# A two-layer Perceiver block on one core: the state-space powers of layer 1's kernel made by VectorE under the end of the first cross-attention

## The chip, the core and the metric

The kernel runs on one core of one Trainium2 chip. A core has engines with queues of their own: PE (TensorE; its weight loads are shown as PEld), DVE (VectorE), ACT (ScalarE), POOL (GpSimd) and SP (SyncE, which here only issues DMAs). They meet through semaphores. The metric is the device time of one execution in microseconds (us); before the change its median over three runs is 2672.54 us.

## The reference, cut to what matters

Two layers, each a cross-attention, a mixing block and a feed-forward block, each added to `x` of 4 x 256 x 256. Three parts matter here.

```python
# layer 0, first block: 16 heads of 16, 256 queries per batch against 4096 context rows
x = x + _L0_xattn_ref(_layernorm(x), ctx_768, ...)       # softmax(q k^T) v, projected
# layer 0, second block: 16 heads of 32, a decayed second-order linear attention
x = x + _L0_attn_ref(_layernorm(x), ...)
# layer 1, first block, contains a state-space convolution whose kernel needs only weights
def s4d(x, log_dt, A_re, A_im, C_re, C_im, D_skip):
    dt = exp(log_dt);  dtA = dt[:, None] * A
    dC = C * (exp(dtA) - 1.0) / A
    powers = exp(dtA[:, :, None] * arange(L))            # L = 256
    K = 2.0 * einsum('dn,dnl->dl', dC, powers).real
```

`K` depends on no activations, so it can be made anywhere ahead of layer 1. The kernel calls "layer 0's" the time in which it makes it; the weights are those of layer 1.

## The kernel before, in words

`program` runs the blocks one after another: `l0_xattn`, `l0_attn`, `l0_ffn`, then layer 1.

`l0_xattn` has 16 units `u`, four batches of four groups of heads. A unit has 16 steps, and each step two halves (`hp` in `step`, two heads each). Two things go on in one step. For unit `u`, PE makes scores (`ps_s`, L444), ACT their exponentials (`e`, L469), and PE adds up values (`o_ps`, L406) in `sums`, one step later. For a unit that is LEAD = 18 steps ahead, PE makes scores in the other layout (`ps_a`, L458) and DVE takes their maxima (`mx`, L473), four `TENSOR_REDUCE`s of 512 columns in a step, two in each half. All of `ps_s` and `ps_a` come from one ring of seven PSUM banks (`ring`); a half takes four of them, in the order score, maxima, score, maxima. A half therefore can't start its scores before the maxima of the half two before it have been read. The last 18 steps have no unit ahead: DVE has only the end of a unit there (`finish`: `o_rec` L173, `on` L174).

Keys and values of a group of eight heads lie in `kts[0]`, `vs[0]` or in `kts[1]`, `vs[1]`; units 14 and 15 use only the second pair. The products that fill them come from `keys` and `values`, which run beside units 0 to 13.

`l0_attn` has 16 units as well. A unit makes scores on PE (`ps_s`, L612), multiplies them by the decay on DVE (`p`, `u`, `z`, L621, six instructions of 768 columns), and makes further products on PE (L632), the last of which ACT copies to `oT` (L641). `first_half` of the next unit is written ahead of `second_half` of this one. Every four units `add_projected` adds to `x`.

Beside these units runs the generator `s4d_kernel`, advanced twice per unit. Its first part makes powers: two exponentials by polynomials, sine and cosine, complex products, and then two tables, `low` (powers 0 to 15) and `high` (16 times as much, with the factor dC), each by four doublings of six instructions, of 128, 256, 512 and 1024 columns. `low` is made by POOL, `high` and everything else by DVE. Its second part makes sums: PE multiplies `low` by `high` (`ps_sn`, L916), DVE masks and reduces (L925, L926), PE transposes (`ps_st`, L937), ACT copies to `s_out`, and SP writes it to `kern`.

Each engine's queue is worked off in order. The order within a queue is not that of the text: the build places instructions by priority and its own estimate of when their inputs and memory are there. (In the trace before, the layer norm of later batches stands among that of the first.) SBUF is handed out in pools; a tile that comes to lie where an older one was waits for the last users of the older one.

The memory for `s4d_kernel` (pool `s4`) is opened after `l0_xattn` and its weights are closed, above that of `l0_ffn`'s weights (`w_f0`).

Of the kernel before, what the change touches and what calls it, by code (L numbers as in the profile page):

```python
# [21 lines left out]
P = 128  # L22
# [222 lines left out]
    return t  # L245


def l0_xattn(c, w):

# [9 lines left out]
    LEAD = 18  # L259
    with ExitStack() as es:  # L260
        one = es.enter_context(tc.tile_pool(name="x0_one", bufs=1))
        ring = es.enter_context(tc.tile_pool(name="x0_ring", bufs=7, space=PSUM))
        acc = es.enter_context(tc.tile_pool(name="x0_acc", bufs=1, space=PSUM))
        two = es.enter_context(tc.tile_pool(name="x0_two", bufs=2))
# [3 lines left out]

        kts, vs, mexps = [], [], []
        for i in range(2):  # L270
            kt = one.tile([P, 2, G], F32, tag=f"kt{i}", name=f"kt{i}")
            kts.append(kt)

            v = one.tile([P, GT * 8 * W + 16], F32, tag=f"v{i}", name=f"v{i}")
            vs.append(v)
            m = one.tile([P, 2, P], F32, tag=f"mexp{i}", name=f"mexp{i}")
            mexps.append(m)
        w.ctxT += [context_keys(c, two, 0, 1), context_keys(c, two, 0, 2, nc.scalar)]
        nc.gpsimd.memset(kts[0][:, 0, :], 1.0)
        mask_rows(c, one, w.mu)  # L280
        nc.vector.memset(kts[0][:, 1, :], 1.0)
# [5 lines left out]
        def keys(b, gp):  # L287

            gs = slice(gp * P, (gp + 1) * P)
            first = (b, gp) == (0, 0)  # L290
            for c4 in range(4):
                ctxT = w.ctxT.pop(0) if w.ctxT else context_keys(c, two, b, c4)
                pss = [bank("ps_k0"), bank("ps_k1")]
                for j, ps in enumerate(pss):
                    nc.tensor.matmul(ps, w.wk[:, 0, gs], ctxT[:, j * 512 : (j + 1) * 512], start=True, stop=False)
                for j, ps in enumerate(pss):
                    hs = slice(64 * j, 64 * j + 64)
                    nc.tensor.matmul(ps, w.wk[hs, 1, gs], ctxT[hs, 1024:1536], start=False, stop=True)  # L298
                ks = two.tile([P, 2, 512], F32, tag="ks", name="ks")
                for j, ps in enumerate(pss):  # L300
                    nc.scalar.copy(ks[:, j, :], ps)  # L301
                for i in range(2):
                    for h in range(4):
                        r = 64 * i + 16 * h
                        ((nc.scalar, nc.gpsimd)[i] if first else nc.sync).dma_start(
                            kts[gp][32 * h : 32 * h + 16, i, c4 * 1024 : (c4 + 1) * 1024],
                            ks[r : r + 16].rearrange("p j n -> p (j n)"),
                        )
                yield

        def values(b, gp):
            v = vs[gp]
            gs = slice(gp * P, (gp + 1) * P)
            for c4 in range(4):
                ctxT = context_keys(c, two, b, c4)
                for i0 in (0, 2):
                    pss = [bank("ps_v0"), bank("ps_v1")]
                    for i in (i0, i0 + 1):
                        ks = slice((i - i0) * P, (i - i0 + 1) * P)
                        for j, ps in enumerate(pss):  # L320
                            k0 = j * 512 + i * P
                            nc.tensor.matmul(ps[:, ks], ctxT[:, k0 : k0 + P], w.wv[:, 0, gs], start=True, stop=False)  # L322
                        for j, ps in enumerate(pss):
                            hs = slice(64 * j, 64 * j + 64)
                            nc.tensor.matmul(  # L325
                                ps[:, ks],
                                ctxT[hs, 1024 + i * P : 1024 + (i + 1) * P],
                                w.wv[hs, 1, gs],
                                start=False,
                                stop=True,  # L330
                            )
# [7 lines left out]

        def tokens(b):  # L340

            xn = row_norm(c, two, "xn", b)
            xnT = two.tile([P, 2, S], F32, tag="xnT", name="xnT")
            ps = bank("ps_t")
            for k in range(2):
                for i in range(2):
# [137 lines left out]
        for t in range(-LEAD, n):  # L484
# [55 lines left out]
def l0_attn(c, w, beside):  # L540
# [9 lines left out]
    with ExitStack() as es:  # L550
# [109 lines left out]
            z = masked_scores(q, wt, 0, "z")  # L660
            return summed([(nu, p), (v, z)], f"oT{u % 4}")

        beside = beside(psum)
        rows = {}
        late = first_half(0)
        oTs = []
        for u in range(16):
            nxt = first_half(u + 1) if u + 1 < 16 else None
# [4 lines left out]
            if u % 4 == 3:  # L673
                add_projected(c, psum, u // 4, oTs, w.wo)
                oTs = []
        for _ in beside:
            pass

def l0_ffn_weights(c, pool):
    w = Ctx()
    w.ga = load_k(c, pool, "f0_ga")
    w.wi = load_k(c, pool, "f0_wi")
    w.wo = load_k(c, pool, "f0_wo")
# [2 lines left out]
    w.bg = load_bc(c, pool, "f0_bg")  # L690
    w.bo = load_bc(c, pool, "f0_bo")
    w.iota = load_bc(c, pool, "iota8")
    return w


def l0_ffn(c, w):
# [111 lines left out]
    v.tensor_tensor(o1, o1, tmp, ALU.add)  # L808


def s4d_kernel(c, pool, psum):

# [16 lines left out]
    ldt = new("ldt")  # L829
    for half in range(2):  # L830
        nc.sync.dma_start(ldt[64 * half : 64 * half + 64, :], c.a["s4_ldt"][half].partition_broadcast(64))
    skip = load(c, pool, "s4_skip", [32, 8])
    own = load(c, pool, "s4_own", [P, P])
    dt = exp_less(c, pool, ldt, 0.0, n2, "s4x")
    re, im = pair("dta")
    v.tensor_tensor(re, ar, dt, ALU.mult)
# [42 lines left out]

    yield  # L880
    low, high = new("low", ns), new("high", ns)
    tmps = [new("tl", [P, 16, 8, 8]), new("th", [P, 16, 8, 8])]

    def groups(t):
        return t.rearrange("p (g e) -> p g e", e=8)

    for i in range(2):
        v.tensor_tensor(high[:, i, :, 0, :], groups(q[i]), groups(n), ALU.mult)
        nc.gpsimd.memset(low[:, i, :, 0, :], 1.0 - i)  # L889
    zs = [pair(f"z{i}") for i in range(9)]  # L890
    zs[0] = z
    for lev in range(8):
        m = 1 << (lev % 4)
        t = low if lev < 4 else high
        if lev == 4:
            v.tensor_scalar(zs[4][1], zs[4][1], -1.0, None, ALU.mult)
        cmul(
            nc.gpsimd if lev < 4 else v,
            [t[:, i, :, m : 2 * m, :] for i in range(2)],
            [t[:, i, :, 0:m, :] for i in range(2)],  # L900
            [groups(p).unsqueeze(2).to_broadcast([P, 16, m, 8]) for p in zs[lev]],
            tmps[lev // 4][:, :, 0:m, :],
        )
# [984 lines left out]
def program(tc, a, out):  # L1888
# [3 lines left out]
    with ExitStack() as es:  # L1892
# [15 lines left out]


        with tc.tile_pool(name="w_a0", bufs=1) as pool_a0:  # L1910
            with tc.tile_pool(name="w_x0", bufs=1, side="right") as pool:
                w = l0_xattn_weights(c, pool)
                l0_xattn(c, w)
                w_a0 = l0_attn_weights(c, pool_a0)
            pool_f0 = es.enter_context(ExitStack())
            w_f0 = l0_ffn_weights(c, pool_f0.enter_context(tc.tile_pool(name="w_f0", bufs=1, side="right")))
            with tc.tile_pool(name="s4", bufs=1, side="right") as pool:
                l0_attn(c, w_a0, partial(s4d_kernel, c, pool))

        with ExitStack() as stack:  # L1920
            w = l1_context_keys(c, stack)
# [145 lines left out]
```

## Time and profile before

| what | value |
|---|---|
| three runs | 2669.84, 2672.54, 2682.69 us |
| profiled execution, time / span | 2677.02 / 2674.9 us |
| mean granted PE clock | 0.929 |
| PE busy, share of the span | 2420.3 us, 90% |
| DVE busy, share of the span | 1618.9 us, 61% |
| ACT busy, share of the span | 1095.0 us, 41% |
| POOL busy, share of the span | 179.1 us, 7% |
| `l0_xattn`, last maxima to last value sum | about 1213.5 to 1276.7 us |
| `l0_attn`, first norm to last addition | about 1276.7 to 1577 us |

Stages are given in microseconds from the start of the span. In the timeline a row has the start, the duration, the engine, the line, the operation with its tiles and a count, and in brackets the idle time ahead of it and what ended it. A row of the table of windows has the window, its length, the busy time of PE, PEld, DVE, ACT and POOL with the number of instructions in parentheses, the granted PE clock (1.00 is full), the DMA share and GB/s. Durations of neighbours on DVE overlap by some 0.08 us, so the cost of one instruction in a full queue is the distance from its start to the next start.

### The profile page before, as it was taken

What the parts mean: (1) busy time and instruction counts of PE and PEld (TensorE: products, weight loads), DVE (VectorE), ACT (ScalarE), POOL (GpSimd) and SP (SyncE); (2) the same over time, 40 slices, a digit from 0 to 9 for tenths busy, and PEclk for the clock granted to TensorE, in tenths of its full rate; (3) what the DMA queues carried; (4) which work ended last, traced back from release to release, by engine and by line L of the source; (5) the groups of instructions that cost most, each with busy time, mean ns of one, the idle gap of its engine ahead of it and who ended that gap; (6) DMA issues with size and microseconds to landing.
All of it is one profiled execution on the core that took longest, in us unless ns stands there. A gap on an engine that the chain in (4) does not pass through costs nothing. (4 is left out here: it accounts for less than half of the span.)

```text
span 2674.9 us, 47755 instructions
## 1 busy us (share of the span) xinstructions
PE 2420.3 (90%) x19345; PEld 1419.5 (53%) x19345; DVE 1618.9 (61%) x3881; ACT 1095.0 (41%) x1913; POOL 179.1 (7%) x202
## 2 busy tenths in 40 slices
PE   8999999999999999999768989888999898984896
PEld 4445454545545454544435544466776777453554
DVE  6655655565565655561784440898798892735554
ACT  1355555555455555556111211555555562010221
POOL 3000000000000000000030000001010011412000
PEclk7899999999999999999888999799999999996876
DMA  7221213121221212100100012210303012100110
GB/s 197 76 53 58 61 50 80 38 73 45 62 56 55 63 37 73 45 2 1 43 1 1 5 47 67 79 60 20 99 22 97 6 50 96 55 0 16 33 24 8
DMA packets 63186, 130.78 MB, mean 49 GB/s; under 512 B 11584, under 2 KB 38912, under 8 KB 62512
## 3 DMA queue, kind: packets, MB, share of 16 engines
q1 hardware_dynamic: 61344, 123.73, 16.4%
q8 instruction: 154, 2.52, 0.4%
q10 hardware_dynamic: 1104, 2.88, 0.4%
q0 software_dynamic: 512, 1.05, 0.2%
q14 instruction: 72, 0.59, 0.1%
HBM read 97.12 MB, written 5.34 MB: 38 GB/s over the span
## 5 line engine op out<-in xcount | busy, mean ns | idle before, releaser
L473 DVE TENSOR_REDUCE mx<-ps_a 128x1 f32<-128x512 f32 x1024 | 658.3, 686 | 436.1 <-PE ps_a L458 436.1
L469 ACT ACTIVATE e<-ps_s 128x512 f32<-128x512 f32 x1024 | 555.8, 594 | 382.5 <-PE ps_a L458 356.5
L458 PE MATMUL ps_a<-kt,qa 32*128 32x512 f32 x2048 | 636.2, 653 | 1.9 <-DMA kt<-ks 0.8
L444 PE MATMUL ps_s<-qb,kt 32*128 32x256 f32 x4096 | 585.9, 401 | 0.0
L444 PEld LDWEIGHTS ps_s<-qb,kt 32*128 32x128 f32 x4096 | 348.7, 184 | 212.4 <-issue 94.2
L406 PE MATMUL o_ps<-e,v 128*32 128x256 f32 x4096 | 327.6, 391 | 0.0
L1152 PEld LDWEIGHTS ps_w<-diag,e 128*128 128x128 f32 x2048 | 238.8, 197 | 23.5 <-issue 21.5
L1152 PE MATMUL ps_w<-diag,e 128*128 128x128 f32 x2048 | 244.5, 281 | 0.4 <-POOL diag L1139 0.4
L458 PEld LDWEIGHTS ps_a<-kt,qa 32*128 32x128 f32 x2048 | 220.6, 186 | 20.9 <-DVE mx L473 7.8
L1109 DVE MAX8 cand<-sc 128x8 f32<-128x128 f32 x1024 | 212.2, 275 | 8.7 <-ACT sc L1097 8.7
L406 PEld LDWEIGHTS o_ps<-e,v 128*32 128x32 f32 x4096 | 81.0, 108 | 239.5 <-issue 229.5
L1133 DVE SCALAR_TENSOR_TENSOR e<-sc,top,e 128x1024 f32<-128x1024 f32 x128 | 159.1, 1279 | 28.5 <-ACT e L1124 28.5
L1124 ACT ACTIVATE e<-sc,neg 128x1024 f32<-128x1024 f32 x128 | 143.1, 1147 | 33.3 <-PE ps_w L1152 29.1
L1097 ACT COPY sc<-ps_s 128x1024 f32<-128x1024 f32 x128 | 126.3, 1007 | 41.9 <-PE ps_s L1088 39.6
L1166 PEld LDWEIGHTS ps_c<-cx,wT 128*128 128x128 f32 x512 | 86.1, 196 | 27.2 <-ACT wT L1160 11.3
L1166 PE MATMUL ps_c<-cx,wT 128*128 128x193 f32 x512 | 97.1, 341 | 1.9 <-ACT wT L1160 1.9
L335 ACT COPY v<-ps_v 128x256 f32<-128x256 f32 x128 | 41.4, 375 | 137.0 <-PE ps_v L325 137.0
L322 PE MATMUL ps_v<-x_wv,ctxT 128*128 128x128 f32 x512 | 92.8, 305 | 0.0
L322 PEld LDWEIGHTS ps_v<-x_wv,ctxT 128*128 128x128 f32 x512 | 69.4, 195 | 35.3 <-DVE mx L473 21.8
L1088 PE MATMUL ps_s<-kt,q 32*128 32x512 f32 x512 | 85.4, 647 | 0.0
L889 POOL MEMSET s_low<- 128x128 f32 x2 | 0.3, 206 | 1241.1 <-DVE x L188 1241.1
L301 ACT COPY ks<-ps_k 128x512 f32<-128x512 f32 x64 | 34.4, 589 | 111.4 <-PE ps_k L298 97.7
(403 smaller groups left out, 2735.6 us busy)
## 6 DMA issues: line engine op xcount, KB each, us to landing
ctxT<-in_ctxT SPq DMA_DIRECT2D x78, 768.0 KB
kt<-ks SPq DMA_DIRECT2D x352, 64.0 KB
cx<-in_ctx SPq DMA_DIRECT2D x16, 768.0 KB
x_w<-in_x_w SPq DMA_DIRECT2D x2, 1024.0 KB
qk<-rot SPq DMA_DIRECT2D x8, 256.0 KB
a_qk<-qk SPq DMA_DIRECT2D x16, 128.0 KB
ctxT<-in_ctxT ACTq DMA_DIRECT2D x2, 768.0 KB
x<-in_x SPq DMA_DIRECT2D x4, 256.0 KB
```

The source lines that it names most:

```text
L322: nc.tensor.matmul(ps[:, ks], ctxT[:, k0 : k0 + P], w.wv[:, 0, gs], start=True, stop=False)
L406: nc.tensor.matmul(o_pss[u][32 * h : 32 * h + 32, :S], vs[g // 2][:, c0 : c0 + 32], ew[h][:, n % 2, :], start=(n == 0), stop=(n == GT - 1),)
L444: nc.tensor.matmul(ps[:, k * S : (k + 1) * S], kts[u % 4 // 2][hs, u % 2, ks], qbs[u][hs, :], start=True, stop=True,)
L458: nc.tensor.matmul(ps, qas[u][hs, tt * P : (tt + 1) * P], kts[u % 4 // 2][hs, u % 2, ch * 512 : (ch + 1) * 512], start=True, stop=True,)
L469: nc.scalar.activation(e, ps.rearrange("p (k n) -> p k n", k=2), AF.Exp)
L473: nc.vector.tensor_reduce(mxs[u][:, tt, h, ch : ch + 1], ps, AX.X, ALU.max)
L1097: nc.scalar.copy(t, ps)
L1109: nc.vector.max(cands[u][:, n, :], sc[u][c4][:, i // 4, (i % 4) * P : (i % 4 + 1) * P])
L1124: nc.scalar.activation(t, src, AF.Exp, bias=neg)
L1133: nc.vector.scalar_tensor_tensor(t, src, top[:, 31:32], t, ALU.is_ge, ALU.mult)
L1152: nc.tensor.matmul(ps[:, i * P : (i + 1) * P], e[c4][:, half, i * P : (i + 1) * P], diag, start=(h == 0), stop=(h == 3),)
L1166: nc.tensor.matmul(ps_c[:, : DC + 1], wT[:, i * P : (i + 1) * P], cxs[b][t][:, j, :], start=(n == 0), stop=(n == 31))
```

## The change

`s4d_kernel` is cut in two. `s4d_powers` makes the tables and is advanced in the last 18 steps of `l0_xattn`; `s4d_sums` runs beside the first units of `l0_attn`. The products of `low` move from POOL to DVE, as do the two `memset`s. So that the tables have memory, `kts[0]`, `vs[0]`, the context, key and norm tiles move to two pools on the right side, which are closed in unit 14 at step 4, and pool `s4` is opened there. The weights of `l0_ffn` are loaded when the sums are done, no longer ahead of `l0_attn`. In `l0_attn` the generator is made after `first_half(0)`, and is no longer run to its end behind the units.

```diff
-def l0_xattn(c, w):
+def l0_xattn(c, w, beside):
...
+        early = es.enter_context(ExitStack())
+        first = early.enter_context(tc.tile_pool(name="x0_first", bufs=1, side="right"))
+        proj = early.enter_context(tc.tile_pool(name="x0_proj", bufs=2, side="right"))
...
-            kt = one.tile([P, 2, G], F32, tag=f"kt{i}", name=f"kt{i}")
+            pool = (first, one)[i]
+            kt = pool.tile([P, 2, G], F32, tag=f"kt{i}", name=f"kt{i}")
...
-            v = one.tile([P, GT * 8 * W + 16], F32, tag=f"v{i}", name=f"v{i}")
+            v = pool.tile([P, GT * 8 * W + 16], F32, tag=f"v{i}", name=f"v{i}")
...
+            if u == 14 and kp == 4:
+                early.close()
+                tail = beside()
+            if ua >= 16 and ka % 2 == 0:
+                next(tail, None)
...
         for _ in range(2):
             sums(0)
+        for _ in tail:
+            pass
...
-        beside = beside(psum)
         rows = {}
         late = first_half(0)
+        beside = beside(psum)
...
-        for _ in beside:
-            pass
...
-def s4d_kernel(c, pool, psum):
+def s4d_powers(c, pool, w):
...
-    tmps = [new("tl", [P, 16, 8, 8]), new("th", [P, 16, 8, 8])]
+    tmps = new("tl", [P, 16, 8, 8])
...
-        nc.gpsimd.memset(low[:, i, :, 0, :], 1.0 - i)
+        v.memset(low[:, i, :, 0, :], 1.0 - i)
...
         cmul(
-            nc.gpsimd if lev < 4 else v,
+            v,
...
-            tmps[lev // 4][:, :, 0:m, :],
+            tmps[:, :, 0:m, :],
         )
+        if m > 2:
+            yield
         if lev < 7:
             cmul(v, zs[lev + 1], zs[lev], zs[lev], tmp)
-        yield
+    yield
+
+    w.low, w.high = low, high
+
+
+def s4d_sums(c, pool, w, psum):
...
-            with tc.tile_pool(name="w_x0", bufs=1, side="right") as pool:
-                w = l0_xattn_weights(c, pool)
-                l0_xattn(c, w)
-                w_a0 = l0_attn_weights(c, pool_a0)
+            pool_x0 = es.enter_context(ExitStack())
+            w = l0_xattn_weights(c, pool_x0.enter_context(tc.tile_pool(name="w_x0", bufs=1, side="right")))
             pool_f0 = es.enter_context(ExitStack())
-            w_f0 = l0_ffn_weights(c, pool_f0.enter_context(tc.tile_pool(name="w_f0", bufs=1, side="right")))
-            with tc.tile_pool(name="s4", bufs=1, side="right") as pool:
-                l0_attn(c, w_a0, partial(s4d_kernel, c, pool))
+            pools, w_s4, w_f0 = [], Ctx(), Ctx()
+
+            def powers():
+                pools.append(pool_x0.enter_context(tc.tile_pool(name="s4", bufs=1, side="right")))
+                return s4d_powers(c, pools[0], w_s4)
+
+            def sums(psum):
+                yield from s4d_sums(c, pools[0], w_s4, psum)
+                pool_x0.close()
+                l0_ffn_weights(c, pool_f0.enter_context(tc.tile_pool(name="w_f0", bufs=1, side="right")), w_f0)
+
+            l0_xattn(c, w, powers)
+            l0_attn(c, l0_attn_weights(c, pool_a0), sums)
```

More of the change, by code (lines that the diff above doesn't have):

```diff
@@ L277, in l0_xattn @@
             mexps.append(m)
-        w.ctxT += [context_keys(c, two, 0, 1), context_keys(c, two, 0, 2, nc.scalar)]
+        w.ctxT += [context_keys(c, proj, 0, 1), context_keys(c, proj, 0, 2, nc.scalar)]
         nc.gpsimd.memset(kts[0][:, 0, :], 1.0)
@@ L289, in keys @@
             gs = slice(gp * P, (gp + 1) * P)
-            first = (b, gp) == (0, 0)
+            start = (b, gp) == (0, 0)
             for c4 in range(4):
-                ctxT = w.ctxT.pop(0) if w.ctxT else context_keys(c, two, b, c4)
+                ctxT = w.ctxT.pop(0) if w.ctxT else context_keys(c, proj, b, c4)
                 pss = [bank("ps_k0"), bank("ps_k1")]
@@ L298, in keys @@
                     nc.tensor.matmul(ps, w.wk[hs, 1, gs], ctxT[hs, 1024:1536], start=False, stop=True)
-                ks = two.tile([P, 2, 512], F32, tag="ks", name="ks")
+                ks = proj.tile([P, 2, 512], F32, tag="ks", name="ks")
                 for j, ps in enumerate(pss):
@@ L304, in keys @@
                         r = 64 * i + 16 * h
-                        ((nc.scalar, nc.gpsimd)[i] if first else nc.sync).dma_start(
+                        ((nc.scalar, nc.gpsimd)[i] if start else nc.sync).dma_start(
                             kts[gp][32 * h : 32 * h + 16, i, c4 * 1024 : (c4 + 1) * 1024],
@@ L314, in values @@
             for c4 in range(4):
-                ctxT = context_keys(c, two, b, c4)
+                ctxT = context_keys(c, proj, b, c4)
                 for i0 in (0, 2):
@@ L340, in tokens @@
         def tokens(b):
-            xn = row_norm(c, two, "xn", b)
-            xnT = two.tile([P, 2, S], F32, tag="xnT", name="xnT")
+            xn = row_norm(c, proj, "xn", b)
+            xnT = proj.tile([P, 2, S], F32, tag="xnT", name="xnT")
             ps = bank("ps_t")
@@ L675, in l0_attn, with l0_ffn_weights @@
                 oTs = []
-        for _ in beside:
-            pass
-def l0_ffn_weights(c, pool):
-    w = Ctx()
+def l0_ffn_weights(c, pool, w):
     w.ga = load_k(c, pool, "f0_ga")
@@ L692, in l0_ffn_weights @@
     w.iota = load_bc(c, pool, "iota8")
-    return w
 def l0_ffn(c, w):
@@ L831, in s4d_kernel @@
         nc.sync.dma_start(ldt[64 * half : 64 * half + 64, :], c.a["s4_ldt"][half].partition_broadcast(64))
-    skip = load(c, pool, "s4_skip", [32, 8])
-    own = load(c, pool, "s4_own", [P, P])
+    w.skip = load(c, pool, "s4_skip", [32, 8])
+    w.own = load(c, pool, "s4_own", [P, P])
     dt = exp_less(c, pool, ldt, 0.0, n2, "s4x")
@@ L901, in s4d_kernel, with new @@
             [groups(p).unsqueeze(2).to_broadcast([P, 16, m, 8]) for p in zs[lev]],
-            tmps[lev // 4][:, :, 0:m, :],
+            tmps[:, :, 0:m, :],
         )
+        if m > 2:
+            yield
         if lev < 7:
             cmul(v, zs[lev + 1], zs[lev], zs[lev], tmp)
-        yield
+    yield
+    w.low, w.high = low, high
+def s4d_sums(c, pool, w, psum):
+    nc = c.nc
+    v = nc.vector
+    low, high, own, skip = w.low, w.high, w.own, w.skip
+    def new(name, shape):
+        return pool.tile(shape, F32, tag="s4_" + name, name="s4_" + name)
     sums = new("sums", [P, 2, 16, 16])
```

## The prediction

> **What bounds the kernel now.** I read, in this order, the costliest groups of the page, the table of windows around the change, and the timelines of DVE, PE and ACT there.
>
> ```profile
> L473 DVE TENSOR_REDUCE mx<-ps_a 128x1 f32<-128x512 f32 x1024 | 658.3, 686 | 436.1 <-PE ps_a L458 436.1
> ```
>
> In the cross-attention the maxima wait for PE: 436.1 us of idle DVE stand ahead of them. PE sets the pace, and DVE has room in small pieces. How much, the windows show: unit 15's maxima, the 18 steps behind them, units 0 to 4 of the attention (the powers), units 5 to 8 (the sums), units 9 to 12 (nothing beside them).
>
> ```profile
> 1168.00:1213.50 45.50, 44.70 (x500) 21.70 (x500) 33.30 (x54) 27.14 (x50) 0.00 (x0) 1.00 0.01 2
> 1213.50:1276.70 63.20, 61.81 (x597) 31.81 (x598) 2.58 (x3) 39.72 (x74) 0.00 (x0) 1.00 0.00 1
> 1276.70:1401.50 124.80, 86.79 (x724) 51.95 (x723) 104.59 (x244) 17.60 (x41) 29.67 (x26) 0.81 0.08 24
> 1401.50:1485.60 84.10, 72.08 (x665) 45.18 (x664) 34.54 (x44) 13.95 (x29) 0.00 (x0) 0.84 0.00 1
> 1485.60:1544.30 58.70, 52.90 (x530) 31.76 (x529) 23.36 (x27) 11.95 (x28) 0.00 (x0) 0.94 0.03 6
> ```
>
> While unit 15's maxima run, DVE is busy for 33.3 of 45.5 us: 12 us are free. In the 18 steps behind them it is busy for 2.6 of 63.2 us: 60 us are free. In the attention with the powers DVE is busy for 104.6 of 124.8 us and PE only for 86.8: DVE bounds that stretch.
>
> **The change: where the powers land.** The text advances them in the last 18 steps. The built program doesn't have them there. In its DVE queue the first power stands behind the 12th of unit 15's 64 maxima and the last in front of the 55th; behind the 64th there is none. The powers are ready as soon as unit 13 lets go of `kts[0]` and `vs[0]`, and the build places them there as filler. This is one half of a step in that queue (in rows from left to right, names shortened):
>
> ```
> L478 TensorReduce mx<-ps_a     L812 tl<-low,z1 128x256     L478 TensorReduce mx<-ps_a
> L813 low<-low,tl 128x256       L814 low<-low,z1 128x256     L815 tl<-low,z1 128x256
> L812 tmp<-z1 128x128           L816 low<-low,tl 128x256     L813 z2<-z2,tmp 128x128
> L814 z2<-z1 128x128            L815 tmp<-z1 128x128         L811 low<-low,z2 128x512
> L478 TensorReduce mx<-ps_a     L478 TensorReduce mx<-ps_a
> ```
>
> A queue is worked off in order, so each pair of maxima now waits for the powers in front of it. PE can't outrun them: a half needs the banks of the maxima two halves back (ring of seven, four a half). So 21 halves run at DVE's pace. Everything in PE's queue (scores, value sums) waits with them.
>
> **Cost of it.** The spacing of maxima and of powers in a full queue:
>
> ```profile
> 1202.68 1.29 DVE L473 TENSOR_REDUCE mx<-ps_a 128x1 f32<-128x512 f32 x2 [0.61 <-PE ps_a L458]
> 1204.32 1.29 DVE L473 TENSOR_REDUCE mx<-ps_a 128x1 f32<-128x512 f32 x2 [0.35 <-PE ps_a L458]
> ...
> 1305.17 0.22 DVE L779 TENSOR_SCALAR s_k<-s_dta 128x128 f32<-128x128 f32 x1
> 1305.30 0.22 DVE L779 TENSOR_SCALAR s4x_k<-s4x_x 128x128 f32<-128x128 f32 x1
> ...
> 1368.14 0.42 DVE L806 TENSOR_TENSOR s_high<-s_high,s_z 128x256 f32<-128x256 f32 x1
> 1368.48 0.42 DVE L805 TENSOR_TENSOR s_high<-s_high,s_th 128x256 f32<-128x256 f32 x1
> 1368.81 0.28 DVE L804 TENSOR_TENSOR s_tmp<-s_z 128x128 f32<-128x128 f32 x1
> 1369.02 0.42 DVE L807 TENSOR_TENSOR s_th<-s_high,s_z 128x256 f32<-128x256 f32 x1
> ```
>
> From start to start: 0.135 us with one tensor input, 0.20 with two (1368.81 to 1369.02), 0.335 at 256 columns; the same timeline gives 0.60 at 512 and 1.13 at 1024, and 0.12 more where an instruction needs the one right ahead of it. The built queue holds 24 of the first kind (3.4 us), 117 of the second (24.0), 12 each of 256, 512 and 1024 columns (4.1, 7.2, 13.6), a reciprocal (0.9) and two memsets (0.2, estimated as one-input instructions), and 26 that need their neighbour (3.1): 56.4 us of powers. The 24 instructions of `low` are in it; POOL needed up to 2.47 us for one of 1024 columns, DVE 1.21.
>
> The 42 maxima of these 21 halves take 0.606 us each (pair 1.29, less the overlap): 25.5 us. Unit 13's reciprocal and product stand among them, 2.0 us. Sum 83.9 us, or 4.0 a half. Before, a half took 1.77 us (1168.24 to 1211.40 is about 24 of them), 37.2 us for 21. Added: 46.7 us. PE's run-ahead gives back one half, 1.8. The eight loads of s4 tables now go out when PE releases `vs[0]`, about 1163.6; with the starts 0.4 us apart and 2.4 us to land, as `s_ldt` had, they land about when they are needed, 1169: 0 to 4 us, I take 1. A cold clock behind the stretch: 1. **Loss 47 us**, of which none is hidden: the 18 steps behind it are bounded by PE (61.8 of 63.2 us) and run as before, with DVE idle.
>
> Two rules bear on this sum. The Trainium skill, "VectorE: DVE Perf Modes", section "The DRAIN you can't avoid", lets the next instruction start only when the one before has left the pipe; then each costs its whole duration, powers 67.7 and maxima 28.8, and the loss is 61. The rows above show starts 0.08 us ahead of the end before, so I take the row and keep 61 for the range. "TensorE: Matmul & The Clock Gate", section "A second HAM failure mode: psum-queue depth-cycling", says that short waits on PSUM banks in each round make the clock fall to one half and back. This trace shows 0.54 in the five microseconds from 1340, where PE waits for DVE. In the stretched halves it would double PE's 1.77 us to 3.54, still below DVE's 4.0: it adds nothing there, by rule or row, but 3 us more if DVE's shortest halves (3.1 us) meet it.
>
> **Gain in the attention.**
>
> ```profile
> 1354.95 2.42 DVE L803 TENSOR_TENSOR s_high<-s_high,s_z 128x128 f32<-128x128 f32 x1
> ...
> 1364.33 1.07 PE L632 MATMUL ps_oT<-z,vn 128*32 128x256 f32 x4 [11.96 <-DVE z L621]
> ```
>
> Beside POOL's products a DVE instruction of 128 columns takes 2.42 us where it takes 0.28 alone, and PE stands for 11.96 us behind a `z` that is queued after such. All this goes. The ends of units 0, 4, 8, 12 and 15 before:
>
> ```profile
> 1322.25 0.37 ACT L641 COPY oT<-ps_oT 128x256 f32<-128x256 f32 x1 [1.20 <-PE ps_oT L632]
> ...
> 1401.10 0.37 ACT L641 COPY oT<-ps_oT 128x256 f32<-128x256 f32 x1 [3.81 <-PE ps_oT L632]
> ...
> 1485.25 0.37 ACT L641 COPY oT<-ps_oT 128x256 f32<-128x256 f32 x1 [3.81 <-PE ps_oT L632]
> ...
> 1543.91 0.37 ACT L641 COPY oT<-ps_oT 128x256 f32<-128x256 f32 x1 [3.81 <-PE ps_oT L632]
> ...
> 1573.35 0.37 ACT L641 COPY oT<-ps_oT 128x256 f32<-128x256 f32 x1 [3.81 <-PE ps_oT L632]
> ```
>
> Four units with nothing beside them take 58.7 us (1485.25 to 1543.91). Unit 0 without powers: PE has both first halves' scores done by 1305.6 and needs 7.2 more, as unit 4 did from 1394.3 to its copy: 1312.8 instead of 1322.3. Then three times 58.7, then 29.4 as before: 1518.3. The sums (PE, DVE, ACT) move from units 5 to 8 to units 0 to 3 and cost what they did, 1485.25 less 1401.10 less 58.7, 25.5 us: 1543.8, a gain of 29.6. Of the 25.5, some 8 were a half-rate clock (0.53 to 0.50 from 1405 to 1420); if that stays away the gain is 37.6. **I take 34.** Bounds: 22, if the sums' two rounds back to back in unit 0 and again in unit 1 close the gate more often, and 42.
>
> **At nothing:** POOL's queue loses 26 instructions and nothing in it waits. The eight loads of `l0_ffn`'s weights, 2.3 MB, move on SP from 1280 to behind the write of `kern`, about 1390; SP has nothing else before 1576, when they are wanted, and before they took about 10 us. Without that cover they would cost those 10. Pools on the other side issue nothing.
>
> **Sum.** +47 - 34 = +13 us. The profiled execution took 2677.0 (span 2674.9), 4.5 above the median; the difference is put on the median: 2672.5 + 13 = **2686 us**. About 0.5%, 13.4 us, is what a measurement of this kernel can tell from no change, so this lies on the edge of it.
>
> **Rivals.** (A) The powers fill DVE's gaps for nothing and the gain stays: 2672.5 - 34 = 2638, faster. For it: DVE has 12 + 60 us free. Against: the 60 lie behind the 64th maximum, where the built queue has no power. It would win if less than about 12 us of powers stood among the maxima; 56 do. (B) DVE costs whole durations, or PE at half clock binds as well: loss 61, 2700. For it: the rule. Against: the rows' overlap. (C) The attention gives little: its PE is near its bound once DVE is out, and the dense sums bring the half clock with them: gain 20, 2700. For it: clock 0.84 in the window of the sums. Against: 38 us of idle PE in the window ahead of that. (D) The change doesn't do what it says: that is the forecast itself, since the powers aren't in the last 18 steps.
>
> **Numbers.** Forecast 0.60, A 0.07, B 0.17, C 0.16. The forecast's own range is 2674 to 2697 (loss 42 to 55, gain 28 to 42), half of it over 2686, none under 2659: 0.30 same, 0.30 slower. B and C are slower. So faster 0.07, same 0.30, slower 0.63. The range leaves out A and the far end of B and C together: 2668 to 2706.
>
> **What would show it.** Right: from about 1164 to 1249 DVE has no idle time, pairs of maxima stand 4 us apart instead of 1.77, PE is busy for less than half (or at half clock); the last 18 steps start at about 1260 instead of 1213.5 and take 63 us again; no POOL products; in the attention units 1 to 4 with the sums take about 76 us (79 before with the powers), units 5 to 8 about 59 (84 before). Wrong: idle DVE among the maxima (loads late, or powers waiting for each other), a PE that keeps its 1.77 us, or sums that make the first units as long as before.

## The result, and the profile after

The changed kernel takes 2682.9 us (median), the kernel before, measured beside it, 2673.4. The ratio is 1.003, 95% interval 1.0018 to 1.0042: 5 to 11 us slower, a small loss where I had forecast 13. Some executions of several kernels below take 30 to 50 us longer, with the 18 steps at half the clock where one of them was traced (e6, e12); the ratios leave these out, unless all executions of a kernel are like that (e1).

The spans of the two profiled executions are 2674.9 and 2681.1 us, 6.2 apart. Two large terms of opposite sign lie under this. The first is in the cross-attention. This is the table of windows of the changed kernel. The rows are: the maxima of unit 15 with the powers among them, its last maxima, the 18 steps behind, units 0 to 4 of the attention, units 5 to 8, units 9 to 12.

```profile
1169.20:1249.70 80.50, 76.93 (x401) 23.18 (x400) 78.75 (x219) 21.79 (x41) 0.00 (x0) 0.58 0.01 3
1249.70:1263.10 13.40, 12.34 (x104) 5.73 (x103) 7.52 (x14) 5.43 (x10) 0.00 (x0) 0.74 0.01 1
1263.10:1326.50 63.40, 62.01 (x599) 31.97 (x598) 2.77 (x4) 39.73 (x74) 0.00 (x0) 1.00 0.00 1
1326.50:1440.80 114.30, 95.35 (x868) 60.21 (x867) 55.51 (x107) 21.47 (x45) 0.00 (x0) 0.91 0.09 25
1440.80:1495.00 54.20, 48.77 (x525) 29.83 (x524) 23.29 (x27) 10.99 (x26) 0.00 (x0) 1.00 0.01 1
1495.00:1552.60 57.60, 52.17 (x527) 31.46 (x526) 23.35 (x27) 11.01 (x27) 0.00 (x0) 0.94 0.00 1
```

DVE is busy for 78.8 of 80.5 us in the first row and for 2.8 of 63.4 in the third: the powers run where the built queue has them, and the 18 steps still have DVE idle. The clock of the first row is 0.58. In the timeline of DVE the maxima stand one by one or in pairs between the powers, and nothing waits but for 1.02 us at 1171, where a table (`ldt`) is still on its way:

```profile
1169.19 1.28 DVE L478 TENSOR_REDUCE mx<-ps_a 128x1 f32<-128x512 f32 x2
1171.49 0.23 DVE L795 TENSOR_SCALAR s4x_x<-s_ldt 128x128 f32<-128x128 f32 x1 [1.02 <-DMA s_ldt<-in_s_ldt]
...
1201.52 0.68 DVE L478 TENSOR_REDUCE mx<-ps_a 128x1 f32<-128x512 f32 x1
1202.12 0.41 DVE L812 TENSOR_TENSOR s_tl<-s_low,s_z 128x256 f32<-128x256 f32 x1
1202.45 0.68 DVE L478 TENSOR_REDUCE mx<-ps_a 128x1 f32<-128x512 f32 x1
...
1203.39 0.42 DVE L814 TENSOR_TENSOR s_low<-s_low,s_z 128x256 f32<-128x256 f32 x1
1203.72 0.42 DVE L815 TENSOR_TENSOR s_tl<-s_low,s_z 128x256 f32<-128x256 f32 x1
...
1251.48 1.29 DVE L478 TENSOR_REDUCE mx<-ps_a 128x1 f32<-128x512 f32 x2 [1.00 <-PE ps_a L463]
1255.06 1.29 DVE L478 TENSOR_REDUCE mx<-ps_a 128x1 f32<-128x512 f32 x2 [2.30 <-PE ps_a L463]
...
1262.26 0.22 DVE L389 TENSOR_REDUCE mexp<-mx 128x8 f32<-128x64 f32 x1
```

`mexp` is where DVE takes the largest of a unit's maxima, once all 64 of its `mx` instructions are done. From unit 14's `mexp` to unit 15's it is 111.9 us (1150.32 to 1262.26), where it was 63.7 (1149.03 to 1212.72): a loss of **48.2 us**. The rows of 1251 and 1255 show the half clock still costing after the powers have ended: now the maxima wait for PE.

Across the whole program the group of the maxima hardly changes, 432.8 us of idle DVE ahead of them instead of 436.1. The cost of this change can't be read from that row, only from the stage:

```profile
L478 DVE TENSOR_REDUCE mx<-ps_a 128x1 f32<-128x512 f32 x1024 | 658.7, 685 | 432.8 <-PE ps_a L463 431.9
```

The other term is in the attention. These are the ends of units 0, 4, 8, 12 and 15 in the timeline of ACT, and ahead of them the reciprocal that ends the cross-attention (DVE's timeline):

```profile
1326.24 1.76 DVE L173 RECIPROCAL o_rec<-den 128x256 f32<-128x256 f32 x1 [49.53 <-PE den L171]
```
```profile
1368.92 0.37 ACT L653 COPY oT<-ps_oT 128x256 f32<-128x256 f32 x1 [3.87 <-PE ps_oT L644]
...
1440.38 0.37 ACT L653 COPY oT<-ps_oT 128x256 f32<-128x256 f32 x1 [3.81 <-PE ps_oT L644]
...
1494.64 0.37 ACT L653 COPY oT<-ps_oT 128x256 f32<-128x256 f32 x1 [3.81 <-PE ps_oT L644]
...
1552.18 0.37 ACT L653 COPY oT<-ps_oT 128x256 f32<-128x256 f32 x1 [3.81 <-PE ps_oT L644]
...
1581.63 0.37 ACT L653 COPY oT<-ps_oT 128x256 f32<-128x256 f32 x1 [3.81 <-PE ps_oT L644]
```

From the reciprocal to the last copy it is 255.4 us, where it was 296.7 (1276.70 to 1573.35): a gain of **41.3 us**. The 18 steps between the two terms take 64.0 us in both. With the 1.3 us by which unit 14's `mexp` already came later, 1.3 + 48.2 - 41.3 = 8.2, which is, but for rounding, how much later the last copy comes. Behind it the changed execution makes up 2.1.

These are two single executions, and the second term varies from one to the next. The stretch takes 63.7 us in all six traces without powers in it, and 111.1 to 111.9 in three with all of them. The attention takes 286.0 to 296.7 us in the five traces that have the code before (those of e7, e8, e9 and e12 with it) and 248.6 to 255.4 in the five that have the changed code (e1, e2, e5, e11). The trace before is the slowest of its five and the changed one the slowest of its own; between the means, 289.9 and 251.6, the gain is 38 us.

### The profile page after: what moved, and what is told of

Its sections match the earlier page's. It is cut to its first block, busy times and chain, and to the rows that moved or that the text cites. A ratio compares the mean times of both kernels' runs of the same rounds, so it can differ in the third digit from the quotient of the medians.

```text
span 2681.1 us, 47776 instructions
## 1 busy us (share of the span) xinstructions
PE 2448.3 (91%) x19345; PEld 1418.8 (53%) x19345; DVE 1611.2 (60%) x3907; ACT 1094.6 (41%) x1913; POOL 148.9 (6%) x176
## 3 DMA queue, kind: packets, MB, share of 16 engines
q1 hardware_dynamic: 61344, 123.73, 16.6%
## 5 line engine op out<-in xcount | busy, mean ns | idle before, releaser
L478 DVE TENSOR_REDUCE mx<-ps_a 128x1 f32<-128x512 f32 x1024 | 658.7, 685 | 432.8 <-PE ps_a L463 431.9
L463 PE MATMUL ps_a<-kt,qa 32*128 32x512 f32 x2048 | 672.5, 670 | 7.1 <-DVE mx L478 3.4
L449 PE MATMUL ps_s<-qb,kt 32*128 32x256 f32 x4096 | 606.6, 412 | 0.0
L449 PEld LDWEIGHTS ps_s<-qb,kt 32*128 32x128 f32 x4096 | 355.2, 188 | 220.0 <-issue 91.4
L411 PE MATMUL o_ps<-e,v 128*32 128x256 f32 x4096 | 336.0, 400 | 0.0
L1177 PEld LDWEIGHTS ps_w<-diag,e 128*128 128x128 f32 x2048 | 238.8, 197 | 23.5 <-issue 21.5
L463 PEld LDWEIGHTS ps_a<-kt,qa 32*128 32x128 f32 x2048 | 230.0, 190 | 38.8 <-DVE mx L478 23.8
L1191 PEld LDWEIGHTS ps_c<-cx,wT 128*128 128x128 f32 x512 | 86.1, 196 | 27.2 <-ACT wT L1185 11.4
L772 POOL TENSOR_TENSOR x<-x,f_bo 128x256 f32<-128x256 f32 x8 | 5.8, 724 | 1645.3 <-DVE x L771 1618.1
```

Of the source, the lines that this page charges most:

```text
L411: nc.tensor.matmul(o_pss[u][32 * h : 32 * h + 32, :S], vs[g // 2][:, c0 : c0 + 32], ew[h][:, n % 2, :], start=(n == 0), stop=(n == GT - 1),)
L449: nc.tensor.matmul(ps[:, k * S : (k + 1) * S], kts[u % 4 // 2][hs, u % 2, ks], qbs[u][hs, :], start=True, stop=True,)
L463: nc.tensor.matmul(ps, qas[u][hs, tt * P : (tt + 1) * P], kts[u % 4 // 2][hs, u % 2, ch * 512 : (ch + 1) * 512], start=True, stop=True,)
L478: nc.vector.tensor_reduce(mxs[u][:, tt, h, ch : ch + 1], ps, AX.X, ALU.max)
L1177: nc.tensor.matmul(ps[:, i * P : (i + 1) * P], e[c4][:, half, i * P : (i + 1) * P], diag, start=(h == 0), stop=(h == 3),)
L1191: nc.tensor.matmul(ps_c[:, : DC + 1], wT[:, i * P : (i + 1) * P], cxs[b][t][:, j, :], start=(n == 0), stop=(n == 31))
```

## The experiments

Three questions: is the loss the place of the powers; what is the gain made of; and, after the first run, why that run gave so little. For the runs in the table the trace gives three stages: the stretch (unit 14's `mexp` to unit 15's), the 18 steps (`mexp` to the last reciprocal) and the attention (reciprocal to the last `oT`).

| kernel | stretch | 18 steps | attention | median us | ratio to before (95%) |
|---|---|---|---|---|---|
| before | 63.7 | 64.0 | 296.7 | 2673.4 | 1 |
| changed | 111.9 | 64.0 | 255.4 | 2682.9 | 1.003 (1.0018 to 1.0042) |
| e1, gate at `mexp` | 64.3 | 101.0 | 252.3 | 2670.7 | 0.9992 (0.998 to 1.0003) |
| e2, upper levels gated | 96.3 | 64.0 | 253.0 | 2672.9 | 0.9984 (0.9968 to 1.0) |
| e3, low table on DVE | 63.7 | 64.0 | 289.8 | 2660.7 | 0.9953 (0.9935 to 0.9972) |
| e4, sums late | 111.6 | 64.0 | 250.3 | 2682.8 | 1.0033 (1.0019 to 1.0046) |
| e5, gate behind unit 14 | 64.3 | 65.7 | 248.6 | 2630.9 | 0.9845 (0.9826 to 0.9863) |
| e10, e5 with sums late | 64.3 | 65.7 | 247.3 | 2631.1 | 0.984 (0.9823 to 0.9858) |
| e11, as e5, gate later | 64.3 | 64.0 | 248.8 | 2632.7 | 0.9853 (0.9836 to 0.9871) |

The median of e2 is over all 14 executions; that of its nine shorter ones (see there) is 2668.6.

**Putting the powers where the text says (e1).**

```diff
     ldt = new("ldt")
...
+    v.scalar_tensor_tensor(ldt, m15[:, 0, :], 0.0, ldt, ALU.mult, ALU.add)
```

`m15` is unit 15's `mexp`, handed to `beside()`. The generator's body first runs behind `with_largest(15)`, so that this is the final `mexp`.

> The changed kernel with one instruction more: behind its load, the first table of the powers is multiplied and added with 0 times unit 15's largest maxima (mexp), so that no power can start before unit 15's 64th maximum. Theory (the loss is the powers' place among the maxima, 48.2 us from the first maximum of unit 15 to mexp; the gain in the attention, 41.3 us, is another matter): the stretch falls back to 60 us, the 18 steps behind it stay at 63 to 65 us because their DVE was idle for 49.5 us in one piece and the powers need 56 of 63, and the time is 2682.9 - 48 = 2635 us, faster than both kernels. Rival 1 (powers slow PE wherever they stand, by the clock or because they overrun the 63 us and hold up unit 14's and 15's ends): the 18 steps grow by 15 us or more, 2650 to 2665. Rival 2 (the loss is the memory given up early, or the loads): nothing changes, 2683.

Measured: the stretch is back at 64.3 us, which answers rival 2: neither the memory given up early nor the loads cost anything there. But the time is 2670.7 us, not 2635. The 18 steps grew to 101 us, the direction of rival 1. Their windows:

```profile
1223.00:1233.00 10.00, 8.30 (x74) 4.03 (x74) 9.69 (x40) 4.95 (x10) 0.00 (x0) 1.00 0.01 2
1233.00:1243.00 10.00, 10.00 (x64) 4.85 (x64) 10.00 (x39) 4.00 (x8) 0.00 (x0) 0.58 0.00 1
1243.00:1253.00 10.00, 10.00 (x56) 4.35 (x56) 10.00 (x18) 3.49 (x7) 0.00 (x0) 0.50 0.01 2
...
1283.00:1293.00 10.00, 10.00 (x58) 4.28 (x51) 0.00 (x0) 4.20 (x8) 0.00 (x0) 0.50 0.00 0
...
1303.00:1313.00 10.00, 10.00 (x62) 4.23 (x58) 0.00 (x0) 3.25 (x6) 0.00 (x0) 0.50 0.00 0
1313.00:1323.00 10.00, 4.50 (x20) 3.38 (x19) 7.22 (x29) 1.95 (x4) 0.00 (x0) 0.84 0.00 0
```

The clock falls to 0.50 at about 1235 and stays there to 1313, long after the powers have ended (1272). PE counts as busy all that time, with half the matmuls in a row. Ahead of the fall PE had three pauses. The first two, 0.81 us behind `mexp` at 1213 and 0.92 us at 1224, are in the kernel before as well. The third is new: in the timeline of PE,

```profile
1224.85 0.70 PE L171 MATMUL den<-o_sb,sel 128*128 128x256 f32 x2 [0.92 <-ACT o_sb L169]
...
1231.85 1.13 PE L449 MATMUL ps_s<-qb,kt 32*128 32x256 f32 x6 [0.78 <-DVE o_rec L173]
```

Unit 14's reciprocal stood behind 16 us of powers in DVE's queue and ran at 1230.04, 16.6 us behind `mexp` instead of 12.2. It is what frees the bank of `den` in the ring, and PE wanted that bank at 1231.1.

**The same without the late reciprocal (e5).**

```diff
     v.tensor_tensor(im, ai, dt, ALU.mult)
     yield
+    yield
+    for t in (re, im):
+        v.scalar_tensor_tensor(t, ons[-1][:, 0:P], 0.0, t, ALU.mult, ALU.add)
```

`ons[-1]` is unit 14's product `on`; the gate of e1 stays.

> The gated kernel again, with one more gate: the first 5.5 us of the powers (up to dta) wait for mexp as before, the other 50 us for unit 14's product on, so that they stand behind unit 14's reciprocal in VectorE's queue instead of in front of it. Theory (in the first gated kernel the half clock from 1235 to 1313 was set off by PE's third pause in 20 us, 0.78 us behind the late reciprocal): without that pause the clock stays at 1.00, the last 18 steps take 63 us instead of 101, the time is 2670.7 - 38 = 2633 us, and the powers end about 1273, ahead of the attention. Rival (56 us of VectorE work beside PE brings the half clock by itself, wherever the reciprocal stands): clock 0.50 again, 2670.

```profile
1223.00:1233.00 10.00, 10.00 (x99) 5.21 (x100) 9.68 (x42) 6.01 (x12) 0.00 (x0) 1.00 0.01 2
1233.00:1243.00 10.00, 10.00 (x100) 5.22 (x102) 9.69 (x44) 6.73 (x14) 0.00 (x0) 1.00 0.01 2
1243.00:1253.00 10.00, 10.00 (x102) 5.22 (x100) 10.00 (x27) 6.73 (x13) 0.00 (x0) 1.00 0.01 2
...
1263.00:1273.00 10.00, 10.00 (x106) 4.94 (x103) 9.97 (x24) 6.52 (x12) 0.00 (x0) 1.00 0.01 2
```

2630.9 us, ratio 0.9845: faster than both kernels. DVE is as full of powers as in e1, PE keeps its 100 matmuls in 10 us and its clock. The powers are hidden but for 1.7 us: the last one, started at 1275.51, holds unit 15's reciprocal up to 1276.65. So the loss of the change is the place of the powers, and in none of e5's five executions did DVE work beside PE bring the half clock by itself.

**Which part of e1 brought it (e7, e8, e9, e12, e11).** e7, e8, e9 and e12 add to the kernel before only idle DVE work between `mexp` and unit 14's reciprocal, and force the reciprocal behind it. The sizes in the list are all that differs.

```diff
                 with_largest(ua)
+                if ua == 15:
+                    t = kts[0][:, 0, 0:1024]
+                    nc.vector.scalar_tensor_tensor(t[:, 0:P], mexps[1][:, 0, :], 0.0, t[:, 0:P], ALU.mult, ALU.add)
+                    for n in [P] * 5 + [1024] * 11:
+                        nc.vector.tensor_tensor(t[:, 0:n], t[:, 0:n], t[:, 0:n], ALU.max)
...
     rec = pool.tile([P, S], F32, tag="o_rec", name="o_rec")
+    if behind is not None:
+        nc.vector.tensor_copy(rec, behind)
```

> The kernel before, with idle VectorE work alone added: a chain of 17 in-place maxima on a free table behind mexp, some 16.5 us, and unit 14's reciprocal put behind it, which is where it stood in the first gated kernel. The powers stay in the attention. Theory (a pause of PE under 1 us behind the late reciprocal sets off the half clock): PE at 0.50 from about 1235 to the end of the cross-attention, 2674 + 38 = 2712 us. Rival (the pause is nothing; the powers' own work did it): the pause alone, 2674 to 2676.

e7 missed its own question. Its reciprocal ran from 1230.63 to 1232.39, but in this build the ring hands PE the bank one half step later, at 1232.5. No pause arose, and 2671.3 us (0.999, 0.9978 to 1.0003) say only that a late reciprocal without a pause costs nothing.

> The kernel before with the idle VectorE chain made 0.86 us longer (17 maxima of which the last has 640 columns), because in the run with the shorter chain unit 14's reciprocal ended 0.15 us before PE needed the bank, so that no pause arose and nothing was tested. Now PE should pause for about 0.75 us at 1232.5, third of three pauses in 20 us as in the first gated kernel. Theory (this pause sets off the half clock for the rest of the 18 steps): 2674 + 38 = 2712 us, in all or most executions. Rival (the pause alone is nothing; powers beside PE, or their order, did it): 2672 to 2676, clock 1.00.

> The same with a chain 2.5 us longer still: PE should pause for 1.6 us at about 1234.2. Theory: half clock to the end of the 18 steps, 2713 us; if the shorter pause left the clock alone and this one doesn't, the length of the pause decides. Rival (no pause of this size matters): 2674 to 2678.

The two pauses, in the timelines of PE of e8 and of e9:

```profile
1233.39 1.13 PE L446 MATMUL ps_s<-qb,kt 32*128 32x256 f32 x8 [0.69 <-DVE o_rec L175]
```
```profile
1236.67 1.13 PE L446 MATMUL ps_s<-qb,kt 32*128 32x256 f32 x8 [1.58 <-DVE o_rec L175]
```

e8: 2672.0 us (0.9996, 0.9982 to 1.001), no half clock in the traced execution, and none of its 20 executions is over 2691: a pause of 0.69 us at that place did nothing, against my theory. e9: the traced execution keeps its clock behind 1.58 us of pause, but three of its eight executions, which were not traced, take 2701 to 2711 us and the others 2666 to 2679.

> The kernel before with a chain of 47 small dependent VectorE instructions of 128 columns between mexp and unit 14's reciprocal, in place of the long ones, so that PE pauses for 0.8 to 1.0 us at the place where it did in the first gated kernel, 6.2 us behind den, and not 7.2 or 9.2 us behind it. No powers beside it. Reading A (the place decides: two pauses of 0.8 us or more within 8 us set off the half clock): 2712 us in all or most executions. Reading B (the pause alone is not enough at any place, it takes the powers that go on behind it): 2674 to 2676 us, clock 1.00.

e12 (`[P] * 46`) puts the pause about where e1 had it. Of 13 executions 12 take 2664 to 2675 us and one 2707. It is the one that was traced, first PE's timeline, then the windows:

```profile
1230.03 1.69 PE L446 MATMUL ps_s<-qb,kt 32*128 32x256 f32 x8 [1.00 <-DVE o_rec L175]
```
```profile
1220.00:1230.00 10.00, 8.10 (x78) 3.82 (x74) 9.05 (x26) 5.69 (x11) 0.00 (x0) 1.00 0.01 2
1230.00:1240.00 10.00, 9.97 (x54) 4.96 (x56) 0.42 (x1) 3.25 (x6) 0.00 (x0) 0.52 0.00 0
1240.00:1250.00 10.00, 10.00 (x56) 4.41 (x58) 0.00 (x0) 3.33 (x7) 0.00 (x0) 0.50 0.01 2
...
1300.00:1310.00 10.00, 10.00 (x54) 4.52 (x52) 0.00 (x0) 3.26 (x6) 0.00 (x0) 0.50 0.00 0
```

The fall comes right behind the pause, with DVE idle from there on, and lasts to the end of the 18 steps (102 us). So a pause can do it with no power beside it, but here only once in 13.

> The first gated kernel with its order of VectorE work kept up to 1227 us (dense powers from mexp on), then unit 14's reciprocal, and the rest of the powers gated behind its product: the reciprocal is 3 us late, but ends about 2 us before PE wants the bank, so PE has no third pause. The two kernels before with a pause alone (0.69 us: clock 1.00 in all executions; 1.58 us: three of eight executions some 35 us longer) leave two readings. Reading 1 (the pause is needed, the powers beside it lower the threshold): clock 1.00, 2631 us. Reading 2 (dense powers from mexp on, or the late reciprocal itself, bring the half clock, the pause is no part of it): clock 0.50, 2670 us.

e11 moves e5's second gate from behind `dta` to behind the sine and cosine, so that DVE's queue is e1's up to 1227 us and the reciprocal is still late, but early enough for PE. In DVE's timeline:

```profile
1229.45 0.23 DVE L861 TENSOR_SCALAR s_cs<-s_cs 128x128 f32<-128x128 f32 x1
1229.59 1.75 DVE L173 RECIPROCAL o_rec<-den 128x256 f32<-128x256 f32 x1
1231.45 0.42 DVE L174 TENSOR_TENSOR on<-o_sb,o_rec 128x256 f32<-128x256 f32 x1
```

Its `mexp` is at 1215.86, 2.4 us after e1's, so this reciprocal is 2.9 us earlier relative to it than e1's, and 1.6 us later than in the kernel before. The clock is 1.00 through all 18 steps, and they take 64.0 us; 2632.7 us, ratio 0.9853, the same as e5. Reading 1 fits: with DVE full of powers but no third pause, none of the 14 executions of e5, e10 and e11 is over 2640 us. All 14 of e1 (2664 to 2675 us) lie some 40 us above e5's; in the two traces 35.3 of these are in the 18 steps and 3.7 in the attention.

A third pause is not needed for the fall, though. e6 (below) has the changed kernel's cross-attention, with nothing on DVE in the 18 steps, and its trace caught a fall. PE's timeline, then the windows:

```profile
1259.40 0.44 PE L394 MATMUL ps_m<-ident,mexp 128*128 128x128 f32 x2 [1.06 <-DVE mexp L389]
```
```profile
1255.00:1260.00 5.00, 3.94 (x44) 1.91 (x43) 3.47 (x7) 2.66 (x6) 0.00 (x0) 1.00 0.01 3
1260.00:1265.00 5.00, 5.00 (x34) 2.23 (x34) 0.30 (x1) 2.17 (x4) 0.00 (x0) 0.60 0.00 0
...
1275.00:1280.00 5.00, 4.51 (x22) 2.07 (x20) 1.33 (x1) 1.36 (x3) 0.00 (x0) 0.50 0.02 3
```

Here the clock falls at about 1261, behind the ordinary pause at unit 15's `mexp`. The changed kernel makes the same pause (1.06 us, at 1262.5) and kept its clock in its trace.

What stays open is what decides. Executions 30 to 50 us longer were 0 of 20, 3 of 8 and 1 of 13 with a late pause without powers (e8, e9, e12), and the powers that go on behind it, or its exact instant, made it 14 of 14 in e1. Where the trace has no third pause, they were 1 of 19 in the changed kernel, 3 of 7 in e6, 5 of 14 in e2, none of 16 in e4, and none of 127 in the kernel before. In all three traces with a fall in the 18 steps it comes 0.5 to 2.8 us behind a pause of 0.78 to 1.06 us. So such a pause can set it off, and taking e1's third pause away cured e1; a rule for when it does is not shown.

**Half a dose (e2).**

```diff
             v.tensor_scalar(zs[4][1], zs[4][1], -1.0, None, ALU.mult)
+            for z4 in zs[4]:
+                v.scalar_tensor_tensor(z4, m15[:, 0, :], 0.0, z4, ALU.mult, ALU.add)
```

> The changed kernel with the same gate put only on the upper levels (the table z of level 4), so that some 17 us of the 56 us of powers stand behind mexp and 39 us stay among the maxima. Theory (the loss is proportional to the DVE time among the maxima): 39 us at the measured density of 2.7 us a half fill 14.6 halves, each 2.2 us longer than PE's pace, loss 33 instead of 48, time 2668 us. Rival (a cost for entering the stretch: loads, half clock, one wait): the loss stays above 43, 2678 to 2683.

The stretch takes 96.3 us, 32.7 more than before; 33 were expected. The loss goes with the DVE time among the maxima, and is not a fixed price for entering the stretch. The ratio, 0.9984 against the changed kernel's 1.003, is 12 us less; 15 were expected. Five of the 14 executions take 2715 to 2717 us, some 47 us more than the others. None of these was traced.

**What the gain is made of (e3, e6, e4).**

e3 is the kernel before with the low table's products on DVE (`nc.gpsimd if lev < 4 else v` becomes `v`) and its two memsets.

> The kernel before with one part of the change alone: the 24 products of the low table and its two memsets on VectorE instead of GpSimd, in the first attention's units as before. Theory (the gain in the attention comes from taking the powers out of it; contention is a part): DVE keeps the powers and gets 13 us more of them, but its small instructions fall from 2.4 to 0.3 us; the attention gains 10 to 25 us of the 41, time 2650 to 2663. Rival 1 (the gain is GpSimd's contention alone): the whole 41, about 2632. Rival 2 (contention doesn't matter, DVE's queue does): 2673 or above, up to 2685.

The contention goes. Two rows of the products in e3's DVE timeline:

```profile
1359.09 1.22 DVE L808 TENSOR_TENSOR s_low<-s_low,s_tl 128x1024 f32<-128x1024 f32 x1
1360.23 0.29 DVE L805 TENSOR_TENSOR s_z<-s_z,s_tmp 128x128 f32<-128x128 f32 x1
```

No product of 128 columns takes 2.42 us there. By the ratio e3 is 7 to 17 us faster than the kernel before, and its median lies in the range of the theory. Its traced execution, at 2671.67 us, was the slowest of six, and the 289.8 us of its attention lie among those of the code before (286.0 to 296.7), so that total decides nothing. The ends of units in ACT's timeline, subtracted, say more (us; a range is over the other traces with the same code):

| attention of | unit 0 | 1 to 4 | 5 to 8 | 9 to 12 | 13 to 15 |
|---|---|---|---|---|---|
| before | 45.6 | 78.9 | 84.2 | 58.7 | 29.4 |
| e7, e8, e9, e12 (code before) | 41.8 to 45.0 | 78.7 to 79.3 | 74.8 to 81.6 | 55.4 to 61.3 | 29.4 |
| e3 | 45.5 | 72.3 | 83.9 | 58.7 | 29.4 |
| changed | 42.7 | 71.5 | 54.3 | 57.5 | 29.4 |
| e1, e2, e5, e11 (code changed) | 42.2 to 49.0 | 66.0 to 68.3 | 54.3 to 55.9 | 54.3 to 57.5 | 29.4 |
| e6, no sums | 34.8 | 55.9 | 54.5 | 54.3 | 29.5 |

Units 1 to 4 of e3 are 6.4 us or more below every trace with the code before, with POOL's 24 products on DVE besides. PE's waits for DVE's `z`, `p` and `u` in the 123 us behind the reciprocal fall from 25 to 28 us to 13.4; in the changed kernel they are 4.4. So part of the gain, 7 to 17 us by the ratio, comes already with the products leaving POOL, and the larger part of the 38 only when the powers leave the attention.

e6 is the changed kernel with the body of `s4d_sums` replaced by a zeroed table.

> The changed kernel with the sums left out: no products of low and high, no masked reductions, no transposes; a zeroed table is written to kern in their place. Its attention stands alone. The forecast put the sums at 25.5 us, of which 8 were a half clock: by it the attention from its first reciprocal to its last copy (255.4 us in the changed kernel) falls to 238 (17.5 less) or 230 (25.5 less), time 2665 or 2657. Rival (my figure for the units without sums, 36.1 + 3 x 58.7 + 29.4 = 241.6, is right, and the sums cost less than either, since they fill PE's waits): 241 to 242, 14 less, time 2669.

In the traced execution the 18 steps ran at half clock, but the attention behind them did not (mean 0.98). Its ends of units:

```profile
1406.85 0.37 ACT L653 COPY oT<-ps_oT 128x256 f32<-128x256 f32 x1 [3.87 <-PE ps_oT L644]
...
1462.74 0.37 ACT L653 COPY oT<-ps_oT 128x256 f32<-128x256 f32 x1 [3.81 <-PE ps_oT L644]
...
1517.25 0.37 ACT L653 COPY oT<-ps_oT 128x256 f32<-128x256 f32 x1 [3.81 <-PE ps_oT L644]
...
1571.51 0.37 ACT L653 COPY oT<-ps_oT 128x256 f32<-128x256 f32 x1 [3.81 <-PE ps_oT L644]
...
1600.97 0.37 ACT L653 COPY oT<-ps_oT 128x256 f32<-128x256 f32 x1 [3.81 <-PE ps_oT L644]
```

The reciprocal is at 1372.06. The bare attention takes **228.9 us**, below both of my figures for it, and four bare units 54.3 to 55.9. The changed kernel's trace has 26.5 us more. By the table some 23 of these lie in units 0 to 4, where the sums run, and 3.3 in units 9 to 12, where none do: there its clock was 0.94. So the sums cost some 23 us. The ratio to before is 0.9947 (0.9927 to 0.9967), 22 us below the changed kernel's, and agrees.

e4 is the changed kernel with `for _ in range(2 if u > 4 else 0)` around the sums' steps, and e10 is e5 with the same line.

> The changed kernel with the sums not advanced in units 0 to 4 but from unit 5 on, as before the change. Theory (the place of the sums doesn't matter: PE, ACT and DVE do the same work for them in any unit): the attention takes 255 us from its first reciprocal to its last copy as in the changed kernel, to within 4 us, time 2683. Rival 1 (my forecast's half: sums beside units 5 to 8 bring the half clock, 8 us): 263 us, 2691. Rival 2 (sums in the early units lie under waits of the pipeline's start, so that late they cost 7 us more or, if the early ones disturb it, less).

> The kernel with the powers behind unit 14's product (2630.9 us), and the sums from unit 5 on as in the kernel with late sums (250.3 us in the attention against 255.4). If late sums are better by themselves, 5 us come off: 2626 us. Rival (the late sums only trade early waits against half clocks; in the whole time they gave nothing, 2682.8 against 2682.9): 2631.

In the traces late sums take 5.1 us off the attention in e4 and 1.3 in e10. Both are within what the changed attention varies by (248.6 to 255.4), and neither is seen in the whole time: 1.0033 against 1.003, 0.984 against 0.9845. Where the sums stand is not worth a change.

## Why the prediction came out as it did

- **The place.** Right. The table of windows shows DVE full from 1169 to 1250 and idle in the 18 steps. e1, e5 and e11 show that the place, nothing else of the change, is the loss.
- **The loss, 47 us.** Right: 48.2. From the 13th to the 55th of unit 15's maxima (1169.19 to 1251.48) it is 82.3 us, where the kernel before takes 37.0, from this row of its DVE timeline to the one of 1204.32:

```profile
1167.37 0.63 DVE L473 TENSOR_REDUCE mx<-ps_a 128x1 f32<-128x512 f32 x1
```

  So this part adds 45.3. I had 83.9 and 1 for the loads, against 37.2. The wait for `ldt` was 1.02 us, and 1.00 was a wait for PE at 1251. Unit 13's reciprocal and product (2.0) stood ahead of the stretch, and the powers took 54.8 us, not 56.4 (the counts and spacings that I printed give 55.7). Behind it, from the 55th maximum to `mexp`, it is 10.8 us instead of 8.4, because the clock was still half: 2.4 where I had taken 1. The remaining 0.5 lies ahead of the stretch; the 1.8 of run-ahead that I subtracted is not to be seen. Several terms were off by 1 to 2 us, in both directions; that the sum came within 1.3 us is in part luck.
- **The two rules.** The starts of 1203.39 and 1203.72 are 0.33 us apart under a duration of 0.42, as in the rows before, and the loss is 48 and not 61. The sentence of "The DRAIN you can't avoid" that I had used doesn't describe these starts; the section goes on to say that an instruction that is not held starts earlier, and early starts are what the rows show. The half clock of "A second HAM failure mode: psum-queue depth-cycling" came (0.58 over the stretch) and added nothing inside it, as reckoned, since DVE did not wait for PE until the powers had ended; what it added came behind.
- **The gain, 34 us.** The mechanism was right, the size was not: 41.3 in the two traces, near my upper bound of 42, and 38 between the means of five. The mis-sized term is "four units with nothing beside them take 58.7 us". I took that window for bare, but it held two half clocks. Before's windows of 2 us in it:

```profile
1519.00:1521.00 2.00, 2.00 (x26) 1.14 (x28) 1.68 (x2) 0.23 (x1) 0.00 (x0) 0.50 0.00 0
...
1535.00:1537.00 2.00, 2.00 (x25) 1.22 (x21) 1.80 (x3) 0.00 (x0) 0.00 (x0) 0.50 0.00 0
```

  The clock of 0.94 in my own row of that window said so, and e7 and e8 have 55.4 there. With e6's units my base of 241.6 becomes 228.9: 12.7 us less, 11.4 of it in the three groups of four units. The sums went the other way: I had taken 21.5, and the changed kernel's trace is 26.5 above e6's, of which 3.3 are a half clock that its units 9 to 12 still had. So 33.6 (which I had rounded to 34) + 12.7 - 5.0 = 41.3. This closes by construction, as the 26.5 is a difference; that the base was too long is what e6 measured.
- **At nothing.** Right. POOL is at 0.00 in every row, and `l0_ffn`'s weights went out at 1423 to 1428 (I had said 1390; the sums end later) and were first read at 1601.
- **The sum.** +47 - 34 = +13 was forecast; +48.2 - 41.3 = +6.9 is in the two traces, +10 with the gain of 38, and 8 us (5 to 11) by the ratio. So 2683 us were measured and 2686 forecast. This is below the 0.5% that I had taken for the limit of what can be told from no change, an outcome to which I gave 0.30 against 0.63 for slower; the interval shows that 0.3% can be told. The error is mostly the gain's.
- **The signs.** They came: DVE without idle time from 1171 to 1250, the 18 steps from 1262 on and 64.0 us long, no products on POOL. Units 1 to 4 took 71.5 us (76 said) and units 5 to 8 54.3 (59 said), both shorter, as the bare units are.
- **The rivals.** A (powers in free gaps, 2638) is not this kernel, and e5 shows that the gaps were there: 2631. But the gate alone, e1, was not enough. No step of mine looked at what else is queued behind powers in the 18 steps. B and C did not happen: no whole durations, PE at half clock did not bind, and the gain was above 20.

## What to carry to other kernels

Filler is placed by when its inputs and its memory are free, not by where the text advances it; read the built queue, and if a stage with room lies later, tie the first instruction to a result of that stage. Then look at what else stands in that queue behind the filler: a short instruction that frees a PSUM bank must go first, since 0.78 us of PE waiting went with 37 us of loss in e1. And before a window is used as the undisturbed base of a sum, look at its granted clock in small slices, and at the same window of a second execution: 0.94 was two half clocks and some 4 us in four units, and the sum used that window three times.

## What the hardware showed that I had not expected

- **The half clock stays.** In e1 it lasted from 1235 to 1313, in e12 from 1231 to 1312 and in e6 from 1261 to 1370, while PE's rows in e1 and e12 say busy 10.00 of 10. A half step took 3.02 us (1235.50 to 1238.52 in e1's PE timeline) instead of 1.63. The Trainium skill, "TensorE: Matmul & The Clock Gate", section "What's actually happening", lets PE come back to full rate after some 3.4 us of sustained work. In these stages the trace differs, and the measurement decides: some 80 us of unbroken work at 0.50. The clock was back at the end of the stage, within 0.7 us of PE's last pause there, in e12 and e6 shortly before it; e6 kept 0.50 across a pause of 0.49 us at 1277. Elsewhere (before at 1519 to 1523) the dip lasted 4 us.
- **The same pauses don't always do it.** From start to start, a pause of 0.69 us 8 us behind one of 0.92 left the clock alone in 20 executions, by their times; one of 1.00 us 6.5 us behind it brought it down once in 13, and one of 0.78 us 7 us behind it, with powers after it, always. In e6 one of 1.06 us was enough, with nothing behind it. No run here shows the rule that decides.
